# Row weighting of layer 0: transposes ahead of the products, and one more pipeline stage

## The chip, the cores and the metric

The kernel runs on one core of a Trainium2 chip. The time is the device time of one execution in microseconds (us); of several runs the median is given. A core has five engines that work through queues of their own: TensorE (PE; its weight loads are shown as PEld), VectorE (DVE), ScalarE (ACT), GpSimd (POOL) and SyncE (SP, here only for issuing DMAs).

## What is computed

Two layers act on 4096 rows of 256 values and a 4096 x 4096 adjacency of ones and zeros. Layer 0, where the change lies, is a graph attention with four heads of 64 columns:

```python
h = jnp.maximum(_layernorm(x, axis=-1), 0.0)
h = (h @ W).reshape(n, heads, head_dim)
src = einsum('nhd,d->nh', h, a[:head_dim, 0])
dst = einsum('nhd,d->nh', h, a[head_dim:, 0])
e = src[:, :, None] + dst.T[None, :, :]
e = where(e > 0, e, ALPHA * e)
attn = softmax(where(adj > 0, e, NEG_INF), axis=-1)
out = einsum('nhm,mhd->nhd', attn, h)
x = x + layernorm(out) * gamma + beta
```

Layer 1 (two steps of diffusion and top-p attention, after another layer norm) follows; the change doesn't touch it, but for a small product of its weights ("merged keys") that is computed early.

## The kernel before

The 4096 rows are 32 blocks of 128. Layer 0 has two stages.

**The weighting stage** (`turn_of`, L295, called for b = 0 to 31) makes of each block the rows that attention sums, weighted by exp(dst) and by exp(0.2 dst), in three bfloat16 parts each. For one block:
- `measured` (L220): VectorE takes mean and variance of the input rows. After every fourth block GpSimd works out scale and shift (`steps`, L140 to L143).
- `opened` (L228): ScalarE applies layer norm and relu (L232), TensorE turns the block with two transposes into PSUM bank 3 or 4 (L235).
- `multiplied` (L237): ScalarE copies the turned block out of PSUM (L239), TensorE multiplies it by W and by the two vectors of logits (L242; four instructions, bank 5, 6 or 7).
- `read` (L244): VectorE copies the logits (L246), ScalarE takes the two exponentials (L249).
- `weighed` (L251): VectorE multiplies the products by them (two instructions, L254).
- `first_part`, `second_part`, `third_part` (L257 to L273): ScalarE casts to bfloat16 (L258); VectorE subtracts that (L262) and ScalarE casts the remainder (L263); VectorE and GpSimd take half each of the last part (L268), GpSimd copies head 0 to where pass 0 reads it (L269), and SP issues the store of the other heads (L270). After every fifth block GpSimd issues a load of adjacency (L174).

The weighted rows of a block lie in one of five buffers, the parts in one of eight slots. `spread` (L275) turns the source logits of four blocks with TensorE and has ScalarE copy them at once (L279). `merged_keys` (L281) does transposes, a copy, products and copies in one turn. `sign_stage` has GpSimd compare source with target logits for the first two pairs of blocks, 1024 columns at a time (L348), at turns 14, 15, 19 and 20; `mask_stage` has VectorE make the masks of those pairs (L358, L359) at turns 30 and 31.

Inside this stage the order of work on VectorE, TensorE, ScalarE and GpSimd is the order in which the code is written (`manual_schedule`): each engine takes its instructions strictly so. SP isn't in that list; the order of its queue is found by the framework.

**The product stage** (the loop at L507) goes over 16 passes (four groups of eight row blocks, four heads) with 16 pairs of blocks each. For pair n it makes signs for n + 3 (ScalarE L352, for two pairs of each pass VectorE L350), masks for n + 2, and 32 matmul instructions into eight PSUM banks (`products`, L369). The turns b = 32 to 34 of the weighting stage, which only finish blocks 29 to 31, run after pairs 1, 2 and 3 (`rest`, L484). Ahead of the loop all logits are turned once more and stored for the later passes (L501 to L504).

Of the kernel before, what the change touches and what calls it, by code (L numbers as in the profile page):

```python
# [22 lines left out]
ALU = mybir.AluOpType  # L23
# [3 lines left out]
P = 128  # L27
# [13 lines left out]
G0 = 8  # L41
# [11 lines left out]
COMPARED = (3, 11)  # L53
# [3 lines left out]
def gat_then_top_p_diffusion(  # L57
# [18 lines left out]
    nc = tc.nc  # L76
# [4 lines left out]
    NB = N // P  # L81
# [79 lines left out]
    with tc.tile_pool(name="l0", bufs=1) as l0, tc.tile_pool(name="l0s", bufs=2) as l0s, tc.tile_pool(name="l0o", bufs=1) as l0o:  # L161
# [21 lines left out]
        def in_bank(i, shape):  # L183
            return pools.ps0.tile(shape, F32, name=f"b{i}", tag=f"acc{i}")

        every = {ET.DVE, ET.PE, ET.Activation, ET.Pool}
        pro = SimpleNamespace(hb={}, pt={}, hT={}, pm={}, uv={}, scales={})
        with tc.manual_schedule(engines=every | {ET.SP}):
            wx = rp.tile([P, KC, D + 2 * H], F32, name="wx", tag="ar", bufs=4)
            a_r, w1_s, w2_s, w1_r, sT = (rp.tile(sh, F32, name=x, tag="hl", bufs=5) for x, sh in (  # L190
# [29 lines left out]
            def measured(b):  # L220
                if b < NB:
                    if b % 4 == 0:
                        pro.mv = l0s.tile([P, 4, nc.vector.BN_AGGR_DIM], F32, name="mv4")
                    moments_of(pro.mv[:, b % 4, :], X[:, b, :])
                    if b % 4 == 3:
                        pro.scales[b // 4] = steps(pro.mv, 4, l0s)

            def opened(b):  # L228
                if b < NB:
                    rs, nmr = pro.scales[b // 4]  # L230
                    hb = pro.hb[b] = l0s.tile([P, D], F32, name="hb", tag="ob")
                    nc.scalar.activation(hb, X[:, b, :], AF.Relu, scale=rs[:, b % 4:b % 4 + 1], bias=nmr[:, b % 4:b % 4 + 1])  # L232
                    pt = pro.pt[b] = in_bank(3 + b % 2, [P, KC, P])
                    for k in range(KC):
                        nc.tensor.transpose(pt[:, k, :], hb[:, ts(k, P)], ident)  # L235
# [21 lines left out]
            def first_part(b):  # L257
                nc.scalar.copy(slots[b % len(slots)][:, :, :, :W1], uvs[b % len(uvs)])  # L258

            def second_part(b):  # L260
                uv, parts = uvs[b % len(uvs)], slots[b % len(slots)]
                nc.vector.tensor_tensor(uv, uv, parts[:, :, :, :W1], ALU.subtract)  # L262
                nc.scalar.copy(parts[:, :, :, ds(W1, W1)], uv)  # L263

            def third_part(b):
                uv, parts = uvs[b % len(uvs)], slots[b % len(slots)]
                for engine, h in ((nc.vector, slice(0, H // 2)), (nc.gpsimd, slice(H // 2, H))):
                    engine.tensor_tensor(parts[:, h, :, ds(2 * W1, W1)], uv[:, h], parts[:, h, :, ds(W1, W1)], ALU.subtract)  # L268
                seen = nc.gpsimd.tensor_copy(ut0[b // QUARTER][:, b % QUARTER], parts[:, 0])  # L269
                nc.sync.dma_start(uv_d[1:, :, b].rearrange("h p t w -> p h t w"), parts[:, 1:])  # L270
                if b % 5 == 1 and len(ax) < 6:
                    with tc.issue_after(seen.ins):
                        ax.append(edges(0, len(ax)))  # L273

            def spread(b):  # L275
                pm = in_bank(b // 4, [P, 512])
                for i in range(4):
                    nc.tensor.transpose(pm[:, ts(i, P)], s_c[:, 0, ds(b - 3 + i, 1)].to_broadcast([P, P]), ident)
                nc.scalar.copy(sr0[:, ds((b - 3) * P, 4 * P)], pm)  # L279

            def merged_keys():  # L281
                pt = in_bank(2, [P, KC, P])
                for k in range(KC):
                    nc.tensor.transpose(pt[:DA, k, :], w1_s[:, k, :], ident)
                nc.scalar.copy(w1_r, pt[:DA])
                for k in range(KC):
                    pm = in_bank(k, [P, 512])
                    nc.tensor.matmul(pm[:, :DA], w1_r[:, k, :], w2_s, start=True, stop=True)
                    nc.scalar.copy(wkq[:, k, DA:], pm[:, :DA])

            def signed(q):
                nc.gpsimd.tensor_scalar(d_big[:, :, ts(q, QUARTER)], d_c[:, :, ts(q, QUARTER)], BIG, None, ALU.mult)
# [1 line left out]

            def turn_of(b):  # L295

                if b < NB:
                    multiplied(b)
                if 0 < b < NB:
                    weighed(b - 1)  # L300
                opened(b + 1)
                if b % 4 == 0 and 0 < b <= G0:
                    spread(b - 1)
                if 0 < b <= NB:
                    first_part(b - 1)
                if 1 < b <= NB + 1:
                    second_part(b - 2)
                if 2 < b <= NB + 2:
                    third_part(b - 3)
                measured(b + 6)  # L310
                if b < NB:
                    read(b)
                if b % QUARTER == 0 and 0 < b < NB:
                    signed(b // QUARTER - 1)
                if b == 12:
                    merged_keys()
                for n, at in enumerate((14, 19)):
                    if at <= b < at + 2:
                        sign_stage(n, b - at)
                if NB - 2 <= b < NB:  # L320
                    mask_stage(b - NB + 2)

        PAIRS = NB // 2
        passes = [(ig, h) for ig in range(NB // G0) for h in range(H)]
# [13 lines left out]
            nc.sync.dma_start(ut, uv_d[passes[k][1], :, ts(q, QUARTER)])  # L338
            shared[k].ut.append(ut)

        def signs(k, p, g=None, only=(0, 1)):

            g = g or l0m.tile([P, 2, G0 * P], U8, name="g", bufs=5)
            h = passes[k][1]
            for c in only:
                j = 2 * p + c
                if len(only) == 1:
                    nc.gpsimd.tensor_scalar(g[:, c, :], shared[k].sr, d_neg[:, h, j:j + 1], 255.0, ALU.is_gt, ALU.mult)  # L348
                elif p in COMPARED:
                    nc.vector.tensor_scalar(g[:, c, :], shared[k].sr, d_neg[:, h, j:j + 1], 255.0, ALU.is_gt, ALU.mult)  # L350
                else:
                    nc.scalar.activation(g[:, c, :], shared[k].sr, AF.Relu, scale=BIG, bias=d_big[:, h, j:j + 1])  # L352
            return g
# [12 lines left out]
                        ax.append(edges(0, len(ax)))  # L366
            return m

        def products(k, p, m):  # L369
            ig, h = passes[k]  # L370
            if p == 0:
                shared[k].acc = [pools.ps0.tile([P, 2, W3 + 1], F32, name=f"acc{i}") for i in range(G0)]
            cols = W3 + (h == 0)
            for i in range(G0):
# [70 lines left out]

        shared[0] = SimpleNamespace(sr=sr0, ut=ut0)

        def sign_stage(n, c=None):
            if n < len(todo):
                k, p = todo[n]  # L450
                gs[n] = signs(k, p) if c is None else signs(k, p, gs.get(n), (c,))

        def mask_stage(n):
            if n < len(todo):
# [26 lines left out]
            nc.vector.tensor_scalar(e_c[i], s_c, (1.0, -1.0)[i] * (1.0 - ALPHA), 0.0, ALU.mult, ALU.min)  # L481
            nc.scalar.activation(e_c[i], e_c[i], AF.Exp)

        rest = {n: lambda b=NB - 1 + n: turn_of(b) for n in (1, 2, 3)}  # L484
        rest.update({4 + i: lambda i=i: factors(i) for i in range(2)})
        with tc.manual_schedule(engines=every):
            for b in range(4):
                measured(b)
            for k in range(KC):
                for i in range(2):  # L490
                    pr = uvs[3 + i][:, :, 0, :HD]
                    nc.vector.tensor_mul(pr, wx[:, k, :D].rearrange("p (h d) -> p h d", h=H),
                                         a_r[:, None, ts(i, HD)].to_broadcast([P, H, HD]))
                    nc.vector.reduce_sum(wx[:, k, ds(D + i * H, H)], pr, axis=AX.X)
            for b in range(4, 6):
                measured(b)
            opened(0)
            for b in range(NB):
                turn_of(b)
            weighed(NB - 1)  # L500
            pt = in_bank(3, [P, KC, P])  # L501
            nc.tensor.transpose(pt[:, 0, :], s_c.rearrange("p h b -> p (h b)"), ident)
            nc.scalar.copy(sT, pt[:, 0, :])
            nc.sync.dma_start(s_d.rearrange("h (b i) -> (h b) i", b=NB), sT)  # L504
            signed(3)
            sign_stage(2)
            for n, (k, p) in enumerate(todo):  # L507
                if n > 0 and p == 0:
                    later.extend(evacuate(k - 1))
                sign_stage(n + 3)  # L510
                mask_stage(n + 2)
                products(k, p, ms.pop(n))
                if n in rest:
                    rest[n]()
                if 1 < p < PAIRS - 3 and later:
                    later.pop(0)()
            later.extend(evacuate(k))
# [854 lines left out]
```

## Time and profile before

| | us |
|---|---|
| median of 3 runs | 2926.36 (2922.95 to 2928.74) |
| the profiled execution | 2926.18 |
| its span on the core | 2924.4 |
| first block's products start (L242) | 11.9 |
| last block's products start (L242) | 112.2 |
| first product of the heads starts (L378) | 115.1 |
| last product of the heads starts (L378) | 820.0 |

Busy over the whole span: PE 2828.4 us (97%), DVE 2196.4 (75%), ACT 1913.3 (65%), POOL 759.9 (26%). In a row of instructions the numbers are start and duration in us, then engine, source line, operation, output and input, and in brackets how long the engine had been idle and who released it. Buffers appear under the name of the memory they share: the weighted rows as `o`, `sr` or `uv`, their parts as `st` or `slots`, PSUM banks as `b`. "A L1 <- B L2" in a list of waits means that engine A at line L1 waited for B's line L2. PEclk is the granted TensorE clock as a share of full speed. A wait is put down to the releaser that came last by the profile.

### The profile page before, as it was taken

The numbers are of one execution on the slowest core, as the hardware profiler recorded it, in microseconds if no ns is written. First come the engines' busy times: TensorE is split into PE (matmuls) and PEld (weight loads), VectorE is DVE, ScalarE is ACT, GpSimd is POOL, SyncE is SP. The second block draws the span as 40 slices with busy tenths as digits, with TensorE's granted clock in tenths as the row PEclk, the third lists the DMA queues.
The fourth block names the chain that finished last, engine by engine and source line by source line (L and its number), as shares of the span: only waits on it lengthen the run. The fifth ranks groups of instructions, "written<-read, shape, count | busy, mean of one in ns | idle before, by whom it ended". The sixth has DMA issues, their size and how long they took to land. (4 is left out here: it accounts for less than half of the span.)

```text
span 2924.4 us, 51961 instructions
## 1 busy us (share of the span) xinstructions
PE 2828.4 (97%) x19033; PEld 2473.4 (85%) x19033; DVE 2196.4 (75%) x5193; ACT 1913.3 (65%) x3063; POOL 759.9 (26%) x1657
## 2 busy tenths in 40 slices
PE   6799999999999999999999999999999999999998
PEld 4699999999977778888888888788778888888887
DVE  6766877768754374788888888442747999999996
ACT  6776787867733634777777776235337777777772
POOL 5501111112010120222333222000103444444442
PEclk7899999999999999999999999999999999999999
DMA  7969578695454784000000000478970000000000
GB/s 162 196 241 238 170 242 182 231 222 190 178 181 163 240 298 158 20 20 20 24 22 20 20 20 18 152 263 280 338 275 22 25 25 25 25 25 29 30 23 22
DMA packets 181147, 368.11 MB, mean 126 GB/s; under 512 B 17168, under 2 KB 133904, under 8 KB 176784
## 3 DMA queue, kind: packets, MB, share of 16 engines
q1 hardware_dynamic: 142352, 270.92, 27.5%
q0 software_dynamic: 21504, 83.89, 12.1%
q10 hardware_dynamic: 17024, 9.85, 1.1%
q8 instruction: 154, 2.52, 0.4%
q14 instruction: 113, 0.93, 0.1%
HBM read 301.35 MB, written 109.38 MB: 140 GB/s over the span
## 5 line engine op out<-in xcount | busy, mean ns | idle before, releaser
L1019 PE MATMUL acc<-X,eT 128*128 128x256 f32 x4096 | 965.8, 381 | 0.0
L1019 PEld LDWEIGHTS acc<-X,eT 128*128 128x128 f32 x4096 | 743.2, 190 | 97.4 <-ACT eT L1013 14.6
L378 PE MATMUL acc<-ut,m 128*128 128x195 bf16 (+1 forms) x8192 | 699.3, 246 | 5.8 <-DVE st L395 5.6
L378 PEld LDWEIGHTS <-m 128*128 128x128 fp8e4 x8192 | 695.4, 97 | 9.6 <-DVE st L395 4.6
L837 ACT ACTIVATE e<-mm,nm 128x1024 f32<-128x1024 f32 x256 | 287.0, 1121 | 311.0 <-PE mm L677 296.5
L352 ACT ACTIVATE g<-sr,d_big 128x1024 uint8<-128x1024 f32 x444 | 467.6, 1141 | 2.6 <-DVE m L358 2.6
L905 DVE SCALAR_TENSOR_TENSOR big<-e,c 128x4096 f32<-128x4096 f32 x58 | 272.9, 4706 | 121.1 <-POOL c L890 84.0
L1013 ACT COPY eT<-tp 128x512 f32<-128x512 f32 x512 | 299.6, 585 | 98.0 <-PE tp L1011 93.5
L861 POOL TENSOR_TENSOR sums<-sums 128x2 f32<-128x2 f32 x64 | 12.6, 198 | 1304.3 <-ACT void L844 1304.3
L577 PE MATMUL mm<-ar,hl 128*128 128x512 f32 x844 | 335.1, 400 | 13.8 <-DMA ar<-adj_d 5.8
L923 DVE MAX8 cand<-big 128x8 f32<-128x228 f32 (+1 forms) x1152 | 348.3, 380 | 0.0
L577 PE MATMUL acc<-ar,hl 128*128 128x512 f32 x844 | 328.1, 392 | 1.5 <-DVE ar L564 1.4
L1011 PE MATMUL tp<-ident,e 128*128 128x128 f32 x2048 | 310.6, 274 | 2.2
L1011 PEld LDWEIGHTS tp<-ident,e 128*128 128x128 f32 x2048 | 248.9, 141 | 70.5 <-ACT eT L1033 27.9
L358 DVE TENSOR_TENSOR m<-g,ax 128x512 uint32<-128x512 uint32 x256 | 182.4, 712 | 115.8 <-PE acc L378 95.8
L948 DVE SCALAR_TENSOR_TENSOR e<-e,found 128x4096 f32<-128x4096 f32 x58 | 259.6, 4477 | 0.0
L844 ACT ACTIVATE void<-e,c1x 128x2048 int8<-128x2048 f32 x128 | 257.5, 2011 | 3.2 <-issue 2.3
L844 ACT ACTIVATE void<-e,c 128x2048 int8<-128x2048 f32 x128 | 257.4, 2011 | 0.0
L577 PEld LDWEIGHTS mm<-ar,hl 128*128 128x128 f32 x844 | 158.9, 188 | 52.0 <-issue 12.8
L677 PE MATMUL mm<-kT,qT 128*128 128x512 f32 x512 | 197.9, 467 | 3.6 <-ACT e L837 2.2
L359 DVE TENSOR_TENSOR m<-m,ax 128x512 uint32<-128x512 uint32 x256 | 177.6, 694 | 26.4 <-DVE m L358 1.4
L577 PEld LDWEIGHTS acc<-ar,hl 128*128 128x128 f32 x844 | 158.9, 188 | 33.7 <-DVE ar L564 2.3
(297 smaller groups left out, 3491.8 us busy)
## 6 DMA issues: line engine op xcount, KB each, us to landing
ar<-adj_d SPq DMA_DIRECT2D x211, 512.0 KB, 4.6
adj_d<-ax POOLq DMA_DIRECT2D x32, 2048.0 KB, 7.1
ut<-uv_d SPq DMA_DIRECT2D x60, 784.0 KB, 5.4
aru<-adj_d SPq DMA_DIRECT2D x45, 512.0 KB, 4.6
ax<-in_adj_t_dram POOLq DMA_DIRECT2D x32, 512.0 KB, 15.7
x<-xf_d SPq DMA_DIRECT2D x78, 128.0 KB, 5.0
xf<-xft_d SPq DMA_DIRECT2D x64, 128.0 KB, 2.2
sr<-s_d SPq DMA_DIRECT2D x15, 512.0 KB, 4.9
```

Source lines behind the costliest of these rows:

```text
L352: nc.scalar.activation(g[:, c, :], shared[k].sr, AF.Relu, scale=BIG, bias=d_big[:, h, j:j + 1])
L378: nc.tensor.matmul(shared[k].acc[i][:, t, :cols], m[t][:, c, ts(i, P)], shared[k].ut[j // QUARTER][:, j % QUARTER, t, :cols], start=(j == ...
L577: nc.tensor.matmul(A.acc[c][s], A.hl[m][:, t, ts(s, P)], A.ar[m][:, ts(c, 512)], start=(j == 0 and t == 0), stop=(j == NB - 1 and t == 1))
L677: nc.tensor.matmul(pm[:, h, :], q[t], kT[:, ds(h * (N // 2) + c * 512, 512)], start=(t == 0), stop=(t == 1))
L837: nc.scalar.activation(ev[:, :, c, :], r.pm[c], AF.Exp, bias=r.nm, accum_out=r.sums[:, c // 2, c % 2:c % 2 + 1])
L844: nc.scalar.activation(void, r.e[:, ts(h, N // 2)], (AF.Relu, AF.Sign)[i], bias=r.c1, scale=-1.0, accum_out=r.sums[:, h, 2 + i:3 + i])
L905: nc.vector.scalar_tensor_tensor(big, r.e, r.c3, r.e, ALU.is_le, ALU.mult, accum_out=r.low3)
L923: nc.vector.max(cand[:, s, :], big[:, edges[s]:edges[s + 1]])
L948: nc.vector.scalar_tensor_tensor(r.e, r.e, r.t, r.e, ALU.is_ge, ALU.mult, accum_out=kept)
L1011: nc.tensor.transpose(pt[:, i, :], r.e[:, ts(4 * g + i, P)], ident)
L1013: nc.scalar.copy(eT, pt)
L1019: nc.tensor.matmul(r.acc[:, 0, :], eT[:, i, :], cur[:, j, :], start=(j == 0), stop=(j == NB - 1))
```

## The change

- `opened` keeps only ScalarE's relu. The transposes are a step of their own, `turned_rows(b + 1)`, first in turn b, ahead of the products of b. Relu runs two blocks ahead, statistics eight (six before).
- Logits and exponentials of block b - 1 are read in turn b, just ahead of its weighting; before, those of b were read at the end of turn b.
- First, second and third part each run one turn later. VectorE's subtraction of the first part is a step of its own (`left`) early in the turn.
- `spread` and the two stages of `merged_keys` issue TensorE's work and return the copies, which ScalarE runs in the next turn (`pro.read`).
- GpSimd's compares are made in eight pieces of 512 columns on the odd turns 13 to 27, in place of four of 1024.
- Masks of pair 0 are made in turn 31, of pair 1 after it (turns 30 and 31 before).
- The logits of all blocks are turned after five of the eight banks of pair 0 (`spread_all`), no longer ahead of it. Four turns, not three, finish among the products.

```diff
-        pro = SimpleNamespace(hb={}, pt={}, hT={}, pm={}, uv={}, scales={})
+        pro = SimpleNamespace(read=lambda: None, hb={}, pt={}, hT={}, pm={}, uv={}, scales={})
...
                     nc.scalar.activation(hb, X[:, b, :], AF.Relu, scale=rs[:, b % 4:b % 4 + 1], bias=nmr[:, b % 4:b % 4 + 1])
+
+            def turned_rows(b):
+                if b < NB:
+                    hb = pro.hb.pop(b)
                     pt = pro.pt[b] = in_bank(3 + b % 2, [P, KC, P])
                     for k in range(KC):
                         nc.tensor.transpose(pt[:, k, :], hb[:, ts(k, P)], ident)
...
+            def left(b):
+                uv = uvs[b % len(uvs)]
+                nc.vector.tensor_tensor(uv, uv, slots[b % len(slots)][:, :, :, :W1], ALU.subtract)
+
             def second_part(b):
-                uv, parts = uvs[b % len(uvs)], slots[b % len(slots)]
-                nc.vector.tensor_tensor(uv, uv, parts[:, :, :, :W1], ALU.subtract)
-                nc.scalar.copy(parts[:, :, :, ds(W1, W1)], uv)
+                nc.scalar.copy(slots[b % len(slots)][:, :, :, ds(W1, W1)], uvs[b % len(uvs)])
...
-                nc.scalar.copy(sr0[:, ds((b - 3) * P, 4 * P)], pm)
-
-            def merged_keys():
-                pt = in_bank(2, [P, KC, P])
+                return lambda: nc.scalar.copy(sr0[:, ds((b - 3) * P, 4 * P)], pm)
+
+            def merged_keys(stage):
+                if stage == 0:
+                    pt = in_bank(2, [P, KC, P])
+                    for k in range(KC):
+                        nc.tensor.transpose(pt[:DA, k, :], w1_s[:, k, :], ident)
+                    return lambda: nc.scalar.copy(w1_r, pt[:DA])
+                pm = [in_bank(k, [P, 512]) for k in range(KC)]
                 for k in range(KC):
-                    nc.tensor.transpose(pt[:DA, k, :], w1_s[:, k, :], ident)
-                nc.scalar.copy(w1_r, pt[:DA])
-                for k in range(KC):
-                    pm = in_bank(k, [P, 512])
-                    nc.tensor.matmul(pm[:, :DA], w1_r[:, k, :], w2_s, start=True, stop=True)
-                    nc.scalar.copy(wkq[:, k, DA:], pm[:, :DA])
+                    nc.tensor.matmul(pm[k][:, :DA], w1_r[:, k, :], w2_s, start=True, stop=True)
+                return lambda: [nc.scalar.copy(wkq[:, k, DA:], pm[k][:, :DA]) for k in range(KC)]
...
             def turn_of(b):
 
+                turned_rows(b + 1)
                 if b < NB:
                     multiplied(b)
-                if 0 < b < NB:
+                if 3 <= b < NB + 3:
+                    left(b - 3)
+                opened(b + 2)
+                pro.read()
+                pro.read = lambda: None
+                if b % 4 == 1 and 1 < b <= G0 + 1:
+                    pro.read = spread(b - 2)
+                if 12 <= b < 14:
+                    pro.read = merged_keys(b - 12)
+                measured(b + 8)
+                if 1 <= b < NB:
+                    read(b - 1)
                     weighed(b - 1)
-                opened(b + 1)
-                if b % 4 == 0 and 0 < b <= G0:
-                    spread(b - 1)
-                if 0 < b <= NB:
-                    first_part(b - 1)
-                if 1 < b <= NB + 1:
-                    second_part(b - 2)
-                if 2 < b <= NB + 2:
-                    third_part(b - 3)
-                measured(b + 6)
-                if b < NB:
-                    read(b)
-                if b % QUARTER == 0 and 0 < b < NB:
+                if 2 <= b < NB + 2:
+                    first_part(b - 2)
+                if 3 <= b < NB + 3:
+                    second_part(b - 3)
+                if 4 <= b:
+                    third_part(b - 4)
+                if b % QUARTER == 1 and 1 < b < NB:
                     signed(b // QUARTER - 1)
-                if b == 12:
-                    merged_keys()
-                for n, at in enumerate((14, 19)):
-                    if at <= b < at + 2:
-                        sign_stage(n, b - at)
-                if NB - 2 <= b < NB:
-                    mask_stage(b - NB + 2)
+                if 13 <= b < 29 and b % 2:
+                    n, piece = divmod((b - 13) // 2, 4)
+                    sign_stage(n, piece)
+                if b == NB - 1:
+                    mask_stage(0)
...
-            for c in only:
+            if piece is not None:
+                c, half = piece // 2, ts(piece % 2, G0 * P // 2)
+                nc.gpsimd.tensor_scalar(g[:, c, half], shared[k].sr[:, half], d_neg[:, h, ds(2 * p + c, 1)], 255.0, ALU.is_gt, ALU.mult)
+                return g
+            for c in range(2):
...
-        rest = {n: lambda b=NB - 1 + n: turn_of(b) for n in (1, 2, 3)}
-        rest.update({4 + i: lambda i=i: factors(i) for i in range(2)})
+        def spread_all():
+            pt = in_bank(7, [P, KC, P])
+            nc.tensor.transpose(pt[:, 0, :], s_c.rearrange("p h b -> p (h b)"), ident)
+            nc.scalar.copy(sT, pt[:, 0, :])
+            nc.sync.dma_start(s_d.rearrange("h (b i) -> (h b) i", b=NB), sT)
+
+        rest = {n: lambda b=NB - 1 + n: turn_of(b) for n in (1, 2, 3, 4)}
+        rest.update({5 + i: lambda i=i: factors(i) for i in range(2)})
...
-            for b in range(4, 6):
+            for b in range(4, 8):
                 measured(b)
             opened(0)
+            turned_rows(0)
+            opened(1)
             for b in range(NB):
                 turn_of(b)
+            read(NB - 1)
             weighed(NB - 1)
-            pt = in_bank(3, [P, KC, P])
-            nc.tensor.transpose(pt[:, 0, :], s_c.rearrange("p h b -> p (h b)"), ident)
-            nc.scalar.copy(sT, pt[:, 0, :])
-            nc.sync.dma_start(s_d.rearrange("h (b i) -> (h b) i", b=NB), sT)
+            mask_stage(1)
             signed(3)
             sign_stage(2)
...
-                products(k, p, ms.pop(n))
+                if n == 0:
+                    products(k, p, ms[n], range(5))
+                    spread_all()
+                    products(k, p, ms.pop(n), range(5, G0))
+                else:
+                    products(k, p, ms.pop(n))
```

More of the change, by code (lines that the diff above doesn't have):

```diff
@@ L339, in weighted, with signs @@
             shared[k].ut.append(ut)
-        def signs(k, p, g=None, only=(0, 1)):
+        def signs(k, p, g=None, piece=None):
             g = g or l0m.tile([P, 2, G0 * P], U8, name="g", bufs=5)
             h = passes[k][1]
-            for c in only:
+            if piece is not None:
[3 more added lines that the diff above has]
+            for c in range(2):
                 j = 2 * p + c
-                if len(only) == 1:
-                    nc.gpsimd.tensor_scalar(g[:, c, :], shared[k].sr, d_neg[:, h, j:j + 1], 255.0, ALU.is_gt, ALU.mult)
-                elif p in COMPARED:
+                if p in COMPARED:
                     nc.vector.tensor_scalar(g[:, c, :], shared[k].sr, d_neg[:, h, j:j + 1], 255.0, ALU.is_gt, ALU.mult)
@@ L367, in masks, with products @@
             return m
-        def products(k, p, m):
+        def products(k, p, m, banks=range(G0)):
             ig, h = passes[k]
-            if p == 0:
+            if p == 0 and banks[0] == 0:
                 shared[k].acc = [pools.ps0.tile([P, 2, W3 + 1], F32, name=f"acc{i}") for i in range(G0)]
             cols = W3 + (h == 0)
-            for i in range(G0):
+            for i in banks:
                 for c in range(2):
@@ L446, in gat_then_top_p_diffusion, with sign_stage @@
         shared[0] = SimpleNamespace(sr=sr0, ut=ut0)
-        def sign_stage(n, c=None):
+        def sign_stage(n, piece=None):
             if n < len(todo):
                 k, p = todo[n]
-                gs[n] = signs(k, p) if c is None else signs(k, p, gs.get(n), (c,))
+                gs[n] = signs(k, p, gs.get(n), piece)
         def mask_stage(n):
```

## Prediction

> **What bounds the kernel now.** I first asked where TensorE stops, with a table of stretches: 11.9 us is the first product of a block, 112.2 the last, and the head products begin at 115.1. Columns: stretch, its length, busy us (and instructions) of each engine, granted clock, DMA share, GB/s.
>
> ```profile
> 11.90:112.20 100.30, 69.44 (x200) 45.66 (x200) 72.02 (x202) 67.74 (x188) 69.65 (x100) 0.71 0.75 157
> 112.20:118.00 5.80, 3.95 (x34) 3.23 (x35) 5.73 (x12) 4.09 (x8) 5.42 (x8) 1.00 1.09 124
> 118.00:156.00 38.00, 38.00 (x450) 38.00 (x448) 28.04 (x43) 31.01 (x33) 5.75 (x7) 1.00 0.90 245
> 156.00:810.00 654.00, 648.43 (x7601) 644.86 (x7599) 487.59 (x907) 498.33 (x587) 89.11 (x134) 1.00 0.70 208
> ```
>
> From 118 us on TensorE has no hole, so whatever the weighting stage gains or loses moves all that follows by as much. In the stage itself no engine is above 72%, so it is bound by waits. Second view, the waits of the stage (12 to 113 us: total, times, longest):
>
> ```profile
> PE b L242 <- ACT hT L239: 25.3, 32, 2.1
> ACT o L249 <- DVE sd_c L246: 11.6, 15, 1.9
> ACT hb L232 <- POOL nmr L143: 7.0, 2, 4.2
> DVE sr L254 <- ACT sr L249: 7.1, 5, 3.1
> DVE sd_c L246 <- PE b L242: 5.4, 8, 1.5
> ACT sr L279 <- PE b L278: 4.2, 2, 2.8
> ```
>
> This is a ring: products wait for ScalarE's copy of the turned rows, that copy stands behind the exponentials of the block before, these wait for VectorE's logits, and these for the products. Third view, one turn in order of time (start, us, engine, line):
>
> ```profile
> 106.15 0.24 ACT L249 ACTIVATE sr<-b 128x4 f32<-128x4 f32 x2 [0.54 <-DVE sd_c L246]
> 106.31 0.37 ACT L239 COPY hT<-b 128x256 f32<-128x256 f32 x1
> ...
> 106.74 2.13 PE L242 MATMUL b<-wx,hT 128*128 128x264 f32 x4 [0.46 <-ACT hT L239]
> 107.17 0.69 DVE L262 TENSOR_TENSOR o<-o,st 128x520 f32<-128x520 f32 x1
> ...
> 108.90 0.17 DVE L246 TENSOR_SCALAR sd_c<-b 128x8 f32<-128x8 f32 x1 [0.70 <-PE b L242]
> 109.17 0.24 ACT L249 ACTIVATE uv<-b 128x4 f32<-128x4 f32 x2 [0.65 <-DVE sd_c L246]
> 109.33 0.37 ACT L239 COPY hT<-b 128x256 f32<-128x256 f32 x1
> ```
>
> Once round takes 3.02 us (106.15 to 109.17); 2.13 of it are four matmul instructions at half clock (they take 1.16 at full clock). On top of the ring lie single stalls: spread logits (1.4 and 2.8), merged keys (about 1), and ScalarE waiting for the layer norm's steps on GpSimd behind the compares (2.75 and 4.21). Together 12 us. From logits of block 3 (22.78) to those of block 30 (111.41) there are 27 turns in 88.6 us, 3.28 each.
>
> **The change part by part.**
>
> *Ring cut.* Logits and exponentials of block b-1 come a turn after its products, and the rows of b+1 are turned before the products of b. The price of a turn is then that of its busiest engine. Dense start-to-start times from the timeline:
> - ScalarE: copy 0.25, relu 0.51, two exponentials 0.12, first and second part 0.51 and 0.53: 1.92 us. The later copy of spread logits or merged keys (0.59, on the turns after the transposes) fits in the slack.
> - TensorE: 1.92 + 0.43 = 2.35 at half clock, 1.2 at full. Block b's products end some 1.6 us before VectorE wants them, so half clock is hidden here; were the turn shorter than 2.35, TensorE would be the bound.
> - VectorE: logits to weighting 0.57 (ScalarE's exponentials lie between; nothing fills this), weighting 0.67, third part 0.34, remainder (`left`) 0.61, statistics 0.45 and 0.10: 2.74. From turn 24 there are no statistics: 2.19.
>
> VectorE sets the turn. In its queue the wait for the exponentials holds up weighting, third part and the next remainder, and ScalarE's second part waits for that; with ScalarE at 1.92 none of it closes a new ring.
>
> *Start.* Statistics of blocks 6 and 7 go ahead (1.1 us); VectorE had 1.55 us idle before the first logits, which hide them; without that they would cost 1.1 once. First logits stay at 14.1; then TensorE at half clock sets 16.4, 18.9; then VectorE without all its stages, 21.3 for block 3 (now 22.78).
>
> *Turns.* 19 x 2.74 + 8 x 2.19 = 69.6 bring block 30's logits to 90.9, if nothing interferes.
>
> *Interference of VectorE and GpSimd.* Today the remainder and third part take 0.69 and 0.42 alone, but in this stage 4.2 us more in sum, when GpSimd's third part or copy runs beside them. GpSimd is busy 69.65 of 100.3 us; the same work in some 84 us meets VectorE more often: 4.2 x 0.83 / 0.69 = 5.0, so 95.9. [...] of 11 such instructions in the four compares of 3.7 to 4.3 us, 9 kept their time and 2 took 0.84 and 0.60 more. I take the row, so nothing is added[...].
>
> *GpSimd's queue.* The four 1024-wide compares (mean 3.94) become eight of half width on the odd turns 13 to 27. A half-width one isn't in the trace: it costs at least 1.85 (half of the shortest, 3.70) and at most 3.94 (if width didn't matter); I take 1.97, since the half-width third part (260) and copy take well under a 1024-wide compare. Behind a compare stand GpSimd's third part (its release of the weighted rows gates the exponentials two turns on), the layer norm's steps and the load issues. For two turns: third parts and copies 2 x 1.08, steps 1.05, load issues and signs 0.55, a compare 1.97, interference 0.6: 6.3 us against VectorE's 5.48 + 0.3 = 5.8. Over eight pairs GpSimd falls 4 us behind; the five buffers forgive about 3 (the exponentials two turns on come 3.8 us after VectorE's own third part, less 0.6 for GpSimd's). Cost 1.2, taken as 1.5: 97.4. The stalls of 2.75 and 4.21 go, because statistics are taken 8 blocks ahead (3 turns from steps to use, not 1.5) and compares no longer come in twos. Next late is that release.
>
> *DMA.* The same packets: 0.75 x 100.3 = 75 us of the DMA engines' time in 84 us. Stores of weighted rows land in 4 to 5 us and their slots are reused after some 16, so this hides; only if stores took over three times as long would it cost. SP's queue gets no new entry ahead of a load that is soon needed; the logits' store comes some 3 us after the products begin, and its reader is six pairs (16 us) later.
>
> *End.* From block 30's logits to the first head product: now 3.70. Then 0.57 + 0.67 + 0.34 + masks 0.84 + 0.69 + 0.1 = 3.2, since the first mask moves into the last turn. So products begin at 100.6, not 115.1: 14.5 gained. Inside the first products: bank 7 waits for ScalarE's logit copy behind two sign instructions (0.3); the third mask comes 0.1 late; 0.26 of today goes. One turn more among the products (remainder, three parts) hides under TensorE's pair of 2.7 us, VectorE needing 1.4 of it for masks; uncovered it would be about 1 us.
>
> *Clock.* [...] In the trace TensorE starts the products at full clock, after two fast turns; after the change it idles some 2 us before them, and fast turns did fall to half clock after 1.27 us idle (103.8 us). [...] I take 0.5.
>
> Sum: 14.5 - 0.3 - 0.1 + 0.26 - 0.5 = 13.9, say 14. The profiled execution took 2926.18 us (span 2924.4 and 1.8 around it), the median is 2926.36; so I take 14 from the median: 2912.
>
> **Rivals.**
> - Full gain: no interference beyond today's noise and no GpSimd backlog. Logits at 90.9, gain about 20.4: 2906. For it: ScalarE and TensorE have slack. Against: VectorE and GpSimd meet more often.
> - GpSimd sets the compare turns moderately: a compare of 2.5 to 2.9 us[...]. 8 x 0.7 more: 8 gained, 2918.
> - The gain is lost again: stores or mask loads late with DMA busy some 90%, holding slots or the first masks for about 10 us: 2922. Against: landing 4 to 5 us, 16 available.
> - Slower, one mechanism: GpSimd's halved compares hardly shrink. At x us per compare the eight pairs lose 8 x (4.36 + x - 5.8) - 3; that eats all 14 at x = 3.6. At the longest compare seen, 4.28, it is 19.7 lost: about 2932. Against it: 3.70 for 1024 columns looks like work per column.
>
> **How the numbers follow.** Chances: main case 0.54 (2908 to 2916), full gain 0.24, moderate GpSimd bound 0.14, lost again 0.05, slower 0.03. Range 2905 to 2919 takes in the first three but their tails. Faster by over 0.2% (5.9 us, about what a measurement of this kernel can tell from no change) means under 2920.5: the first three, 0.92; within it 0.05; slower 0.03.
>
> **What would show it.** Right: about 2.8 us from logits to logits, the wait of products for the copy of turned rows nearly gone, first head product near 100 us, everything after shifted alike. VectorE waits for exponentials stay near 0.45 a turn. Wrong: ScalarE's exponentials waiting for GpSimd's third part over turns 14 to 28 (GpSimd bound), half-width compares well over 2 us[...], holes in TensorE between 100 and 120 us.

## The result and the profile after

| | before | after |
|---|---|---|
| median us (7 runs each) | 2927.92 (2922.95 to 2931.18) | 2915.40 (2914.26 to 2918.28) |
| ratio of the runs | | 0.9962 (0.9952 to 0.9972) |
| profiled execution, its span | 2926.18, 2924.4 | 2918.28, 2916.5 |
| logits of block 3, of block 30 | 22.78, 111.41 | 21.36, 99.32 |
| last product of the heads starts | 820.0 | 809.1 |

The change is faster by 0.38%, 11.1 us by the ratio, 12.5 by the medians; forecast were 14 us and 2912, range 2905 to 2919. The last head product comes 10.9 us earlier; the profiled span is only 7.9 us shorter, because the stages after it took 3.0 us longer in this execution. A second profile of the same kernel (r1 below) has the last head product at 809.2 and a span of 2912.1. In these two executions the last head product repeats within a tenth of a microsecond, while the stages after it differ by 4.5 us. Below, the last head product is used beside the time; it isn't always that steady (e2 and e10, one kernel, differ by 2.3 us).

The table of stretches. The first runs again from the first to the last block's products; the others end where the second mask of pair 0 is ready, after the first twenty head products, and at 156 us. Columns as before: stretch, length, busy us of PE, PEld, DVE, ACT and POOL, granted clock, DMA share, GB/s.

```profile
12.30:98.20 85.90, 61.97 (x200) 42.36 (x199) 68.90 (x198) 61.85 (x183) 71.36 (x100) 0.75 0.82 167
98.20:103.10 4.90, 2.43 (x6) 1.24 (x6) 4.44 (x9) 1.27 (x4) 4.87 (x7) 0.50 1.06 257
103.10:106.10 3.00, 3.00 (x21) 2.80 (x22) 2.53 (x6) 2.31 (x4) 2.84 (x5) 0.56 1.07 85
106.10:156.00 49.90, 49.90 (x589) 49.90 (x587) 39.10 (x71) 42.90 (x52) 8.46 (x10) 1.00 0.94 269
```

The first stretch is 14.4 us shorter with nearly the same work (VectorE 68.9 us busy, 72.0 before; GpSimd 71.4, 69.7): mostly waiting went. Part of the 14.4 is only that a block's products now come a turn ahead of its logits; by the logits of block 31 (114.74 and 102.96) the stage ends 11.8 us earlier. GpSimd is now busy 83% of the stretch, VectorE 80%. And the products begin at a granted clock of 0.50 to 0.56; before, at 1.00.

The waits of the stage (12 to 113 us: total, times, longest):

```profile
PE b L246 <- ACT hT L243: 23.9, 25, 1.8
ACT o L253 <- DVE sd_c L250: 14.7, 16, 2.4
...
POOL rs L140 <- DVE mv L149: 3.1, 1, 3.1
ACT o L253 <- POOL slots L274: 3.0, 3, 1.2
...
ACT slots L269 <- DVE uv L266: 1.5, 1, 1.5
ACT uv L253 <- DVE sd_c L250: 1.5, 3, 0.7
ACT uv L253 <- POOL st L274: 1.5, 2, 1.0
...
ACT hb L232 <- POOL nmr L143: 0.3, 1, 0.3
```

TensorE's wait for the copy has hardly fallen (25.3 before), yet it no longer matters: VectorE waited for products only once in this stage, for 0.4 us, where it had 5.4. A large wait of an engine that runs ahead is slack. ScalarE's waits for spread logits (4.2) are gone, and of those for the layer norm's steps (7.0) 0.3 is left. New is ScalarE waiting for GpSimd's third part (L274).

One full turn on VectorE, in order of time, from logits (L250) to logits:

```profile
38.03 0.14 DVE L250 TENSOR_SCALAR sd_c<-b 128x8 f32<-128x8 f32 x1
38.61 0.76 DVE L258 TENSOR_TENSOR uv<-b,uv 128x256 f32<-128x256 f32 x2 [0.44 <-ACT uv L253]
39.28 0.42 DVE L274 TENSOR_TENSOR slots<-o,slots 128x260 bf16<-128x260 f32 x1
39.62 0.69 DVE L266 TENSOR_TENSOR sr<-sr,st 128x520 f32<-128x520 f32 x1
40.23 0.42 DVE L148 BATCH_NORM_STATS2 st<-X 128x6 f32<-128x256 f32 x1
40.69 0.18 DVE L149 BATCH_NORM_AGGREGATE mv<-st 128x2 f32<-128x6 f32 x1
40.78 0.14 DVE L250 TENSOR_SCALAR sd_c<-b 128x8 f32<-128x8 f32 x1
```

2.75 us, with one hole of 0.44. This is the turn the prediction worked out (2.74).

### The profile page after: what moved, and what is told of

The parts are those of the page before. It is cut to its first block, busy times and chain, and to the rows that moved or that the text cites. A ratio compares the mean times of both kernels' runs of the same rounds, so it can differ in the third digit from the quotient of the medians.

```text
span 2916.5 us, 51977 instructions
## 1 busy us (share of the span) xinstructions
PE 2828.3 (97%) x19033; PEld 2475.8 (85%) x19033; DVE 2196.8 (75%) x5193; ACT 1908.9 (65%) x3063; POOL 763.6 (26%) x1661
## 5 line engine op out<-in xcount | busy, mean ns | idle before, releaser
L885 POOL TENSOR_TENSOR sums<-sums 128x2 f32<-128x2 f32 x64 | 12.5, 196 | 1309.0 <-ACT void L868 1309.0
```

## The experiments

"Last head product" is when the last product of the heads starts in that run's trace. Stretch is by how much VectorE's remainders and third parts, up to the logits of block 31, took longer than 0.69 and 0.42 in sum (4.5 in the kernel before by this count). The runs were made on several chips; the ratio is always to the kernel before on the same chip. Times in the text are from one trace of each run.

| run | median us | ratio (95%) | logits 30 | last head product | stretch |
|---|---|---|---|---|---|
| change | 2915.40 | 0.9962 (0.9952 to 0.9972) | 99.3 | 809.1 | 5.2 |
| r1, change again | 2916.20 | 0.9967 (0.9954 to 0.9980) | 98.6 | 809.2 | 5.2 |
| e1, compares on ScalarE | 2912.73 | 0.9961 (0.9947 to 0.9975) | 93.3 | 803.3 | 2.6 |
| e2, GpSimd side alone | 2923.63 | 0.9998 (0.9990 to 1.0007) | 103.5 | 814.2 | 5.2 |
| e10, the same again | 2924.03 | 0.9996 (0.9988 to 1.0005) | 105.6 | 816.5 | 5.2 |
| e3, remainder in the gap | 2908.72 | 0.9949 (0.9935 to 0.9962) | 92.3 | 803.8 | 6.8 |
| e4, wide compares | 2919.08 | 0.9980 (0.9973 to 0.9988) | 101.1 | 809.7 | 4.6 |
| e7, copies at once | 2923.11 | 0.9991 (0.9983 to 0.9999) | 103.1 | 814.2 | 4.8 |
| e6, twelve transposes | 2914.65 | 0.9959 (0.9946 to 0.9971) | 98.6 | 808.7 | 5.1 |
| e5, e1 and e3 together | 2904.96 | 0.9929 (0.9916 to 0.9942) | 85.8 | 796.8 | 8.7 |
| e9, e5 and copy on ScalarE | 2905.56 | 0.9932 (0.9918 to 0.9946) | 89.0 | 798.6 | 4.4 |
| e8, e5 and 32 transposes | 2900.19 | 0.9915 (0.9902 to 0.9929) | 86.1 | 795.3 | 8.5 |
| e11, e8 and earlier masks | 2901.90 | 0.9925 (0.9912 to 0.9939) | 87.2 | 793.7 | 8.3 |

Theory: once the ring is cut, VectorE sets the turn; GpSimd costs some 8 us on top, by stretching VectorE's instructions and by a backlog. Rivals: GpSimd's side is the whole gain, or something other than VectorE sets the turn.

**r1: the change again.**

> The changed kernel itself, to stand beside the next three on one chip, and as a second trace of it. All theories: ratio to before 0.996 as already measured; logits of block 30 at 99 us, 77 to 79 us after those of block 3; if the trace differs by several us from the first one in this stage, the meetings of GpSimd and VectorE vary from execution to execution.

77.9 us from block 3 to block 30 (78.0 in the first trace), last head product 809.2 (809.1): as expected.

**e1: compares on ScalarE.**

```diff
-nc.gpsimd.tensor_scalar(g[:, c, half], sr[:, half], d_neg[...], 255.0, ALU.is_gt, ALU.mult)
+nc.scalar.activation(g[:, c, half], sr[:, half], AF.Relu, scale=BIG, bias=d_big[...])
```

(shortened; issued right after `pro.read()`.)

> The changed kernel with its eight half-width compares moved from GpSimd to ScalarE, ahead of the exponentials. Theory (VectorE sets the turn; GpSimd's backlog from turn 20 on and its meetings with VectorE take some 8 us): GpSimd has slack, the exponentials no longer wait for its third part (3.1 us in the changed kernel), and about half of the 5.1 us by which remainders and third parts are stretched goes. Logits of block 30 near 94.5 us instead of 99.3, gain 4 to 5: about 2911 us. Rival (the stretch comes from third parts and copies alone, and the backlog hides): logits within 1 us, 2915. Rival (ScalarE is the next bound): 1.92 + 0.6 a turn is under 2.74, so not before turn 24; if it were, slower than 2915.

Logits of block 30 came at 93.3, 6.0 us earlier (expected 4.8). The exponentials' waits for GpSimd left no more than 0.3 us of delay to VectorE (3.1 in the change), and the stretch halved to 2.6. Both parts of GpSimd's cost are shown in the trace, and ScalarE had the room. The time, with this chip's ratio of 0.9961, doesn't show the gain over the change that the trace has.

**e2 and e10: the GpSimd side alone**, in the kernel before (statistics of blocks 6 and 7 go ahead as well; the edit is shortened).

```diff
-                measured(b + 6)
+                measured(b + 8)
...
-                for n, at in enumerate((14, 19)):
-                    if at <= b < at + 2:
-                        sign_stage(n, b - at)
+                if 13 <= b < 29 and b % 2:
+                    n, piece = divmod((b - 13) // 2, 4)
+                    sign_stage(n, piece)
```

> The kernel before with only the GpSimd side of the change: statistics eight blocks ahead, eight half-width compares on the odd turns 13 to 27. The ring of products, logits, exponentials and copy stays. Theory: only the two waits for the layer norm's steps go (2.75 and 4.21), the turn stays at 3.0 us: gain 6 to 7, about 2921 us. Rival (the GpSimd side is the whole gain, the ring cut gives nothing that the engines don't take back): about 2916. Rival (the ring cut alone gives it): within 2 us of before, 2927.

> The GpSimd side of the change alone, once more (statistics eight ahead, eight half-width compares, in the kernel before), because its first trace had the last head product 5.8 us earlier than the kernel before, and its time only 0 to 3 us less. Theory (the gain in the stage is real and alike in every execution; the later stages scatter by some us): the trace again shows the last head product near 814 us, the time 3 to 6 us under before. Rival (the stage itself varies and the first trace was a lucky one): last head product at 817 or later, time within 2 us of before.

From logits of block 3 to those of block 30 the two traces took 81.7 and 82.3 us, against 88.6 before and 78.0 in the change: the 7 us of step waits are gone, the ring stays. But their last head products lie 5.8 and 3.5 us ahead of the kernel before, and the times only 0.6 and 1.2 us by the ratios. That GpSimd's side is the whole gain is refuted by the time. The stage isn't as alike from execution to execution as the theory had it: block 3's logits came at 21.7 and 23.4. In e2 TensorE was at full clock from the third block on (its products take 1.16 us at 17.57 and 19.85), in e10 still at half (2.13 us at 18.20 and 21.22), and there these products set the pace: e10's logits waited for products at 17.35, 20.36 and 23.38, 3.0 us apart, where e2's came at 19.13 and 21.74, 2.6 us apart, without such a wait. The time shows less than the traces in e1, e2, e4, e5, e7, e10 and e11, by 2 to 5 us. Part of this is that in all of these but e5 the traced execution lay 1 to 4 us under the median of its run (e2: 2919.51, the lowest of 13); the rest, at most 3.6 us (e11), stays open.

**e3: the remainder in the gap.**

```diff
-                if 3 <= b < NB + 3:
-                    left(b - 3)
                 opened(b + 2)
...
                     read(b - 1)
+                if 3 <= b < NB + 3:
+                    left(b - 3)
+                if 1 <= b < NB:
                     weighed(b - 1)
```

> The changed kernel with VectorE's remainder (0.61) moved between the logits and the weighting, where VectorE waits 0.45 for the exponentials. Theory (VectorE sets the turn at 2.74 until GpSimd takes over in the compare turns): turns 5 to 13 take 2.3 us, from there GpSimd holds them near 2.85: logits of block 30 some 4 us earlier, about 2911 us. Rival (GpSimd never bounds): all 27 turns gain 0.44, 12 us, 2904. Rival (something else than VectorE sets the turn): within 1 us, 2915.

VectorE in order of time, one turn:

```profile
27.39 0.14 DVE L250 TENSOR_SCALAR sd_c<-b 128x8 f32<-128x8 f32 x1
27.45 0.69 DVE L266 TENSOR_TENSOR uv<-uv,slots 128x520 f32<-128x520 f32 x1
28.05 0.75 DVE L258 TENSOR_TENSOR o<-b,o 128x256 f32<-128x256 f32 x2
28.72 0.42 DVE L274 TENSOR_TENSOR st<-sr,st 128x260 bf16<-128x260 f32 x1
29.05 0.42 DVE L148 BATCH_NORM_STATS2 st<-X 128x6 f32<-128x256 f32 x1
29.51 0.18 DVE L149 BATCH_NORM_AGGREGATE mv<-st 128x2 f32<-128x6 f32 x1
29.61 0.14 DVE L250 TENSOR_SCALAR sd_c<-b 128x8 f32<-128x8 f32 x1
```

The hole is gone and the turn takes 2.22, in place of 2.75. From block 3 to block 12 the trace needs 21.8 us, the change 25.2: VectorE set the turn. From block 12 to 30 it gains only 2.5 us more, and ScalarE's waits for GpSimd's third part rise to 5.7 us at the line that had 3.0: GpSimd takes over there, as expected, but costs less than expected: logits of block 30 came 7 us earlier, not 4.

**e4: wide compares**, in the changed kernel.

```diff
-                if 13 <= b < 29 and b % 2:
-                    n, piece = divmod((b - 13) // 2, 4)
-                    sign_stage(n, piece)
+                for n, at in enumerate((14, 19)):
+                    if at <= b < at + 2:
+                        sign_stage(n, b - at)
...
-                c, half = piece // 2, ts(piece % 2, G0 * P // 2)
+                c, half = piece, slice(0, G0 * P)
```

> The changed kernel with the four compares of 1024 columns at turns 14, 15, 19 and 20, as before, in place of eight halves. Theory (GpSimd's third part gates the exponentials two turns on, with some 3 us forgiven): two of 3.9 in successive turns put GpSimd some 6.5 us behind, so the exponentials wait 3 to 4 us twice, against 3.1 in sum in the changed kernel: 3 to 5 us slower than it, about 2919. Rival (only the sum of GpSimd's work counts, not its pieces): the same, 2915.

Waits of its stage:

```profile
ACT o L253 <- POOL st L274: 4.4, 2, 2.9
ACT o L253 <- POOL slots L274: 4.2, 1, 4.2
```

As expected, two long waits (2.9 and 4.2 the longest) stand where the change had several near 1; block 30 comes 2 us later. The last head product is only 0.6 us later, because the first products ran at full clock here (nineteen in 1.79 us, 3.05 in the change; rows under e6 and e8). By the ratios (0.9980 against 0.9962 and 0.9967) halves are worth 4 to 5 us, as expected; by the last head products less, so their size stays loose.

**e7: copies at once.**

```diff
-                    pro.read = spread(b - 2)
+                    spread(b - 2)()
-                    pro.read = merged_keys(b - 12)
+                    merged_keys(b - 12)()
```

> The changed kernel with ScalarE's copies of the spread logits and merged keys made at once, in the turn of TensorE's work, as before. Theory (VectorE sets the turn, ScalarE has 0.8 us of slack): the copy waits for products and transposes of its own turn, 1 to 2 us past the exponentials' time, twice for logits and about once in sum for the keys: 3 to 5 us slower than the changed kernel, all before turn 14. Rival (the slack hides it): within 1 us.

Block 12's logits came at 49.7, in the change at 46.6; the last head product 5.1 us later. By the ratios it is 7 to 8.5 us. Theory right: making these copies a turn later is worth 5 us or more, about half of the whole change. Beside e2 this says more. e7 cuts the ring and has GpSimd's side, e2 has GpSimd's side alone, and they end alike: 81.9 and 81.7 us from block 3 to block 30, last head product 814.2 in both, intervals of the ratio that overlap. Without the later copies, cutting the ring gained nothing that these runs can show.

**e6 and e8: TensorE kept busy.** In turns 30 and 31 after the products of the block, into bank 2, with 2 and 10 (e6) or 2 and 30 (e8) transposes:

```diff
+                if NB - 2 <= b < NB:
+                    idle = in_bank(2, [P, KC, P])
+                    for i in range((2, 10)[b - NB + 2]):
+                        nc.tensor.transpose(idle[:, i % KC, :], ident, ident)
```

> The changed kernel with twelve needless transposes of the identity into a free bank during turns 30 and 31, so that TensorE isn't idle before the first head products. Theory (these ran at half clock because of the idle time: granted clock 0.50 at 102 to 105 us, 19 instructions in 3.05 us): at full clock they take 1.7, so the first pair ends 1.3 us earlier; in the time about 1 us, which the timing hardly shows, so the trace decides. Rival (the clock depends on the load of a longer stretch, which twelve transposes don't change): the 20 first instructions again take 3 us. Other side: the transposes delay the last block's products by up to 0.5.

> Both edits (compares on ScalarE, remainder in the gap) and 2 + 30 needless transposes in turns 30 and 31, so that TensorE works up to the first head products; twelve left it idle for 1.8 us again, and the first twenty products took 2.7 us in place of 3.3. Theory (idle time of some 2 us before the products halves the clock): now they take 1.7 to 1.9 at a granted clock of 1.00, the last head product comes at 795.3 or 1.5 us ahead of the run with both edits alone. Rival (it is not the idle time): 3 us again and nothing gained; if the clock is already half when the thirty begin, they take 6 us and delay the products by 2 to 3.

Twelve transposes ended 1.8 us before the masks, and the first products took 2.7 us: no decision. TensorE around the gap ahead of the first head products, in the change, in r1 and in e4:

```profile
98.15 2.13 PE L246 MATMUL b<-wx,hT 128*128 128x264 f32 x4 [0.46 <-ACT hT L243]
102.18 0.34 PE L391 MATMUL acc<-ut,m 128*128 128x196 bf16 x1 [1.90 <-DVE m L371]
103.09 3.05 PE L391 MATMUL acc<-ut,m 128*128 128x196 bf16 x19 [0.57 <-DVE m L372]
```

```profile
97.47 1.16 PE L246 MATMUL b<-wx,hT 128*128 128x264 f32 x4 [1.42 <-ACT hT L243]
101.50 0.35 PE L391 MATMUL acc<-ut,m 128*128 128x196 bf16 x1 [2.87 <-DVE m L371]
102.42 3.29 PE L391 MATMUL acc<-ut,m 128*128 128x196 bf16 x19 [0.57 <-DVE m L372]
```

```profile
100.74 1.16 PE L246 MATMUL b<-wx,hT 128*128 128x264 f32 x4 [0.49 <-ACT hT L243]
103.94 0.26 PE L391 MATMUL acc<-ut,m 128*128 128x196 bf16 x1 [2.04 <-DVE m L371]
104.86 1.79 PE L391 MATMUL acc<-ut,m 128*128 128x196 bf16 x19 [0.66 <-DVE m L372]
```

The four product instructions of the last block take 1.16 us at full clock. In the change they take 2.13: its clock was at half before the gap began (granted 0.50 from 92.2 us on). In r1 it fell inside the gap (products of 1.16 us before it, 0.35 for the first head product after it, 0.26 in e4), and in e4 it stayed full (nineteen in 1.79 us). TensorE at the start of the products in e5 (without transposes), then in e8:

```profile
89.12 0.35 PE L392 MATMUL acc<-ut,m 128*128 128x196 bf16 x1 [2.25 <-DVE m L372]
90.03 3.29 PE L392 MATMUL acc<-ut,m 128*128 128x196 bf16 x19 [0.56 <-DVE m L373]
```

```profile
86.95 3.44 PE L310 MATMUL b<-ident 128*128 128x128 f32 x30
90.23 1.87 PE L396 MATMUL acc<-ut,m 128*128 128x196 bf16 x20
```

And their granted clock (the number after the busy times), e5 over its first products, e8 over its own:

```profile
90.00:93.30 3.30, 3.27 (x20) 3.03 (x21) 2.83 (x7) 2.31 (x4) 3.15 (x6) 0.50 1.12 175
```

```profile
89.10:92.00 2.90, 2.90 (x33) 2.83 (x32) 2.43 (x6) 1.58 (x4) 2.83 (x5) 1.00 1.11 260
```

Without an idle gap the same work takes 1.87 us at full clock (granted 1.00, where e5 had 0.50), and the last head product comes 1.5 us earlier. With the gap filled the clock stayed full in both runs that filled it: in e11, whose transposes also run up to the products, twenty take 1.90 us. That the length of the gap decides is not shown: e4 kept full clock over 2.04 us idle and 0.66 more, e5 lost it over 2.25 and 0.56, and r1 kept it over an earlier 1.85 us (products of 1.16 us after it) in which the change (1.84, then 2.13) lost it. The load of a longer stretch remains a rival.

**e5: both edits.**

> The changed kernel with both edits: compares on ScalarE, and VectorE's remainder between logits and weighting. Theory (the turn is that of the busiest engine): VectorE 2.3, TensorE 2.35 at half clock, ScalarE 1.92 and 2.5 on the odd turns with a compare, GpSimd about 2.0: 27 turns at 2.4 and some 3 us of stretch, logits of block 30 near 88 us, 10 us under the changed kernel, about 2905 us. Rival (gains of the two overlap, since each removes GpSimd from the path in its own way): as the better of the two alone, 2909.

Logits of block 30 at 85.8 (expected 88), time as expected. The gains of e1 and e3 add up: 6.0 and 7.1 alone, 13.5 together. VectorE now works 97% of the stage (63.67 of 65.8 us from 20 to 85.8), but some 8 us of that is stretch.

**e9: GpSimd's copy of head 0 on ScalarE**, a turn later, on top of e5:

```diff
-                seen = nc.gpsimd.tensor_copy(ut0[b // QUARTER][:, b % QUARTER], parts[:, 0])
+                if b >= NB - 4:
+                    seen = nc.gpsimd.tensor_copy(ut0[b // QUARTER][:, b % QUARTER], parts[:, 0])
...
+                if 0 <= b - 5 < NB - 4:
+                    nc.scalar.copy(ut0[(b - 5) // QUARTER][:, (b - 5) % QUARTER], slots[(b - 5) % len(slots)][:, 0])
```

> Both edits, and GpSimd's copy of head 0 moved to ScalarE a turn later (blocks 0 to 27). Theory (VectorE's remainder and third part are stretched, 8.7 us in sum, by GpSimd's third part and copy, about half each): the stretch falls to about 4.5, but ScalarE has 1.92 + 0.5 a turn and 3.0 on the eight turns with a compare, 0.6 over VectorE's: about even, 2903 to 2906. Rival (copy takes no part in the stretch): the stretch stays at 8 to 9, and the time rises by ScalarE's 4 to 5 us.

The stretch fell from 8.7 (e5) to 4.4, as expected if GpSimd's copy makes half of it (the turns are longer too, so the share is no more than an indication). Block 30 came 3.2 us later and the time is about even: ScalarE has become the limit, busy 68.96 of the 68.99 us from 20 to block 30.

**e11: masks of pair 0 a turn earlier**, on top of e8 with 2 and 6 transposes.

```diff
-                if b == NB - 1:
+                if b == NB - 2:
                     mask_stage(0)
```

> The fastest so far (compares on ScalarE, remainder in the gap, TensorE kept busy) with the masks of pair 0 made in turn 30, not 31, and 2 + 6 needless transposes instead of 2 + 30. Theory (the first head products wait only for these masks, which stand on VectorE behind everything of turn 31): logits of block 30 come 1.5 us later, but the products can begin 0.7 us after them and not 4.2, and then wait about 1 us for the last weighting and the next masks: last head product 1 us earlier, near 794.3. Rival (the masks cost VectorE the same wherever they stand, and the last weighting sets the end): within 0.5 us of 795.3, or later.

```profile
87.17 1.90 PE L396 MATMUL acc<-ut,m 128*128 128x196 bf16 x20
89.05 0.33 PE L504 MATMUL b<-ident,sd_c 128*128 128x128 f32 x1
89.21 0.50 PE L396 MATMUL acc<-ut,m 128*128 128x196 bf16 x4
90.24 0.51 PE L396 MATMUL acc<-ut,m 128*128 128x196 bf16 x4 [0.53 <-DVE o L258]
91.60 6.57 PE L396 MATMUL acc<-ut,m 128*128 128x196 bf16 x73 [0.84 <-ACT sT L505]
```

Products begin 3.1 us earlier than in e8, give back 0.53 to the last weighting and 0.84 to the logit copy, and the last head product comes 1.6 us earlier: the theory. The time can't tell it from e8 (the intervals overlap). e8 has the lowest median, 0.85% under the kernel before.

## Why the prediction was right, and where its sizes were off

- *What bounds, and the ring.* Right: the stage was bound by waits, and all that follows shifted (10.9 us at the last head product). The ring cut needs the later copies: without them (e7) it ends like GpSimd's side alone (e2), and neither has the gain of the whole. The ring cut without GpSimd's side was not run.
- *VectorE's turn of 2.74.* Right: 2.75 in the trace, and moving one item into the hole of 0.44 takes it to 2.22 (e3). Block 3 at 21.3 forecast, 21.36 measured; that it is so exact is luck, r1 has 20.76.
- *Interference.* Forecast 5.0, measured 5.2. The prediction added nothing for meetings with a compare, since 9 of 11 in its trace cost nothing, and so it was again for most: 15 remainders and third parts began inside one of the eight, and 14 stayed within 0.1 of their usual time (0.69 and 0.42); the fifteenth took 1.95 us, most of it after the compare, beside GpSimd's third part and copy. But it does happen: in e2 two of 13 took 0.41 and 0.24 us more beside a compare alone. That GpSimd's copy has a share in the stretch is indicated by e9 (8.7 to 4.4).
- *GpSimd's queue: mis-sized.* Forecast 1.5, measured 3.1 (waits of weightings beyond 0.44). The compare was about right (1.97 forecast, 2.0 to 2.7 measured). What failed is the comparison with VectorE: I set GpSimd's pair of turns against 5.8 us over all eight pairs, but from turn 24 VectorE has no statistics and asks for 2.19 a turn, while GpSimd, by then 4.5 us behind, still has the compares of turns 23, 25 and 27 to run (82.93, 88.72 and 92.88 us). Four of the five long waits stand there; the fifth, 0.4 of the 3.1 us, is in turn 22. VectorE:

```profile
82.75 0.76 DVE L258 TENSOR_TENSOR uv<-b,uv 128x256 f32<-128x256 f32 x2 [0.95 <-POOL st L274]
...
85.94 0.76 DVE L258 TENSOR_TENSOR o<-b,o 128x256 f32<-128x256 f32 x2 [1.35 <-POOL slots L274]
...
91.72 0.76 DVE L258 TENSOR_TENSOR o<-b,o 128x256 f32<-128x256 f32 x2 [1.34 <-POOL slots L274]
...
96.88 0.76 DVE L258 TENSOR_TENSOR uv<-b,uv 128x256 f32<-128x256 f32 x2 [0.80 <-POOL st L274]
```

  and GpSimd in the same time, without a hole:

```profile
82.93 2.01 POOL L358 TENSOR_SCALAR g<-sr,d_neg 128x512 uint8<-128x512 f32 x1
84.91 0.67 POOL L274 TENSOR_TENSOR slots<-o,slots 128x260 bf16<-128x260 f32 x1
85.52 0.51 POOL L275 COPY ut<-slots 128x392 bf16<-128x392 bf16 x1
85.99 0.66 POOL L274 TENSOR_TENSOR slots<-o,slots 128x260 bf16<-128x260 f32 x1
```

  The third part that ends at 85.58 released ScalarE's exponentials at 85.61, and these VectorE's weighting at 85.94.
- *End: mis-sized.* Forecast 3.2 us from block 30's logits to the products; the first instruction came after 2.86, the rest after 3.77, since the masks took 1.21 and 0.88 beside GpSimd's late third part and copy, not 0.84 and 0.69. The wait of bank 7 (0.3) and the late third mask (0.1) did not appear.
- *Clock: mis-sized, and in this trace not by the gap named.* The 0.5 was an estimate that no trace gave; 19 instructions took 3.05 us, and 1.79 in e4 at full clock: 1.3. The prediction let the clock fall in the 2 us ahead of the products. In this trace it fell ten microseconds before, in 1.84 us idle ahead of 92.99 (granted 1.00 from 91.8 to 92.0, 0.50 from 92.2 on); in r1 it did fall in the gap, of 2.87 us. In e4 a gap of 2.04 us and 0.66 more left it full. No length of idle time at which it falls can be read from these runs.
- *Sum.* 1.6 (GpSimd) + 0.2 (stretch) + 0.6 (masks) + 0.8 (clock) - 0.4 (bank 7, mask) = 2.8 of the 3.0 us that separate 13.9 from 10.9.
- *Rivals.* 2915.4 lies in the main case (2908 to 2916), at its upper edge. What the rival "GpSimd sets the compare turns moderately" describes did happen, later in the stage and at about a quarter of its extra price (1.6 us, where 14 less 8 is 6). The slower rival's sum counts 1.5 us twice: its loss was set against 14, which already has that much for GpSimd in it. Right would be 3.75 us per compare, and 2931.
- *DMA.* Share 0.82 in the stage and no wait of the engines there for a store: right.
- *The sign that would show it.* "The wait of products for the copy nearly gone" was a wrong sign: it stayed at 23.9 us as slack.

## What to carry to other kernels

When a stage is bound by a ring of waits, the worth of cutting it is the ring's time less the dense time of the busiest engine, and that engine's queue is then read turn by turn: a hole between an instruction and its answer from another engine is filled by moving an independent item into it (e3, 7 us for one moved step). That worth comes out only if nothing else waits in the same turn: here the copies had to move as well (e7). An engine that is off the path has to be sized against the shortest turn of the others, not the mean one, or its backlog comes out at the end. Waits of the engine that runs ahead are no sign of anything; ask who waits for it.

## What the runs showed of the hardware

- Beside GpSimd's third part or copy VectorE's remainders took up to 1.95 us in the change (0.69 alone; this one began in the last 0.3 us of a compare, the others reached 1.17) and its third parts up to 0.79 (0.42 alone); in e5, where GpSimd makes no compares, the longest were 1.64 and 0.85. Beside its compares of 512 columns most kept their time (14 of 15 within 0.1 us in the change, 11 of 13 in e2).
- In six traces TensorE came to a gap of 1.60 to 2.87 us ahead of the head products at full clock (the last block's products took 1.16 us), and nineteen head products after it took 2.71 to 3.29 us (r1, e1, e3, e5, e6, e9; the granted clock of e5 was 0.50 in them); in e4, after 2.04 us, they took 1.79. With 32 needless transposes in turns 30 and 31 the granted clock was 1.00 there, and the last head product came 1.5 us earlier (e8 against e5).
